# The second FFN of a two-layer vision block on one Trainium2 core: eight experts' probabilities spread by DMA, weighted inputs on GpSimd

## The chip, the core and the metric

The kernel runs on one core of a Trainium2 chip, in one launch, with fp32 data. The core has a matrix engine (TensorE, PE in the profile; PEld is its loading of weights), VectorE (DVE), ScalarE (ACT), GpSimd (POOL), and SyncE (SP), which here does nothing but issue DMA transfers. Every engine works through its own queue in a fixed order and waits at an instruction until its inputs and its buffer are ready. The metric is the device time of the whole kernel in microseconds, median of three runs.

## What is computed

The reference is a network of two layers on an input of 8 images with 128 channels and 64 x 64 points. Layer 0 is a four-way selective scan and a mixture of 64 experts. Layer 1 is a cascade of small state-space blocks with a convolutional FFN, and then, on the tokens, a mixture of eight experts. Only the end of layer 1 matters here:

```python
h1 = jnp.einsum('bchw,oc->bohw', out, fc1_w) + fc1_b[None, :, None, None]
dw = jax.lax.conv_general_dilated(h1, dw_w, (1, 1), 'SAME', ...)   # 3 x 3, each channel alone
h2 = jax.nn.gelu(dw + dw_b[None, :, None, None])
ffn = jnp.einsum('bohw,co->bchw', h2, fc2_w) + fc2_b[None, :, None, None]
return out + ffn
...
def _L1_ffn_ref(x, router_w, router_b, expert_w, expert_b):        # x: normalised tokens
    router_probs = jax.nn.softmax(x @ router_w + router_b, axis=-1)
    top_p, top_i = jax.lax.top_k(router_probs, 2)
    top_p = top_p / jnp.sum(top_p, axis=-1, keepdims=True)
    expert_out = jnp.einsum('bnd,edc->bnec', x, expert_w) + expert_b
    gathered = jnp.take_along_axis(expert_out, top_i[..., None], axis=2)
    return jnp.einsum('bnk,bnkc->bnc', top_p, gathered)
```

The kernel computes all eight experts for every token, with a probability of zero for the six that are not chosen: output = sum over e of (x * p_e) W_e, plus the biases weighted by p.

## The kernel before

`second_ffn` does the convolutional FFN and the mixture in one software pipeline. Its unit is a tile of 128 channels x 512 tokens (`S`), 64 of them (8 images of 8 tiles). A list `steps` gives each stage a delay in tiles; at every tick the stages run from the last to the first, each on another tile:

- `load` fetches `ys`, `seed` and `x2` (named `x` in the profile) from DRAM;
- `center`, `scale`: a norm (products `ln_m`, `ln_v` with the mean matrix; VectorE subtracts, giving `xc`; ScalarE squares, giving `sq`; GpSimd multiplies), and GpSimd adds into `seed`;
- `hidden`: product `h_p`, which ScalarE moves into rows `h`;
- `taps`: the 3 x 3 convolution as 18 VectorE instructions into two PSUM banks `dw`;
- `feed`: ScalarE's gelu, product `f_p`, VectorE and GpSimd add, giving `res`;
- `center2`, `scale2`: the second norm, giving `yn`;
- `logits`: four products of `yn` with the router for each tile into one PSUM bank `lg`, which holds a group of four tiles (`RS`). After the fourth, `route` reads the bank (`e<-lg_p`) and finds the two largest of eight and their normalised weights `pw` in some twenty small VectorE instructions;
- `weights`, for one tile: four transposes (`pt_p`, in the same bank `lg`), ScalarE copies them to rows 0 to 7 of `pT`; four rows are stored to DRAM (`p_d`) and read back spread over 128 partitions (`pb`, 1 MB);
- `weighted`: GpSimd multiplies `yn` with each of the four spread rows, giving four tiles `xwd`;
- `experts`: a bias product from `pT`, then eight products summed in bank `o_p`. For experts 0 to 3 the probability is spread by a product `pb_p` with a selection matrix `sel8`, and VectorE multiplies `yn` with it (`xw`); experts 4 to 7 use `xwd`. The two kinds alternate. VectorE adds `o_p` to `res`, and SP stores it.

All DMAs are issued by SP, in one order. The framework puts each engine's instructions in order by a plan with its own costs, so the order on an engine is not that of the source: tiles of different stages are mixed. A pool with `bufs=n` has n buffers by name, and an instruction that needs one waits until the earlier user is done. The bank `lg` has one buffer. The logits of a group occupy it over four tiles, and only when `route` has read it can the transposes of the group before go, so the work of `weights` comes in bursts of four tiles.

In the profile most VectorE and GpSimd instructions carry the lines of helpers (L335 `tt`, L341 `ts`, L344 `stt`), products L288, ScalarE L296; the names of tiles tell them apart.

Of the kernel before, what the change touches and what calls it, by code (L numbers as in the profile page):

```python
# [9 lines left out]
F32 = mybir.dt.float32  # L10
BF16 = mybir.dt.bfloat16
AF = mybir.ActivationFunctionType
ALU = mybir.AluOpType
# [10 lines left out]
S = 512  # L24
# [245 lines left out]
def bc(ap, n, axis=None):  # L270

    axis = len(ap.shape) if axis is None else axis
    v = ap.unsqueeze(axis)
    shape = list(v.shape)
    shape[axis] = n
    return v.to_broadcast(shape)


class Net:
# [809 lines left out]
    def ssd_project(self, cfg, W, ring, stk, n_tok, wk, ps):  # L1089
# [3 lines left out]
        nc = self.nc  # L1093
        NP, G, nh, hd, hi, ds = cfg.np, cfg.g, cfg.nh, cfg.hd, cfg.hi, cfg.ds
        g2, NH, gh, pb, pz = cfg.g2, cfg.nhalf, cfg.gh, cfg.pb, cfg.pz
# [8 lines left out]
        silus = []  # L1104
        BC = wk.tile([pb, NP, 2, n_tok], F32, name=f"BC_{t_}", bufs=nb_)
        per = min(NP, S // n_tok)
        for j0 in range(0, NP, per):
            p = ps.tile([128, 2, S], F32, tag="a", bufs=self.wide, name="bc_p")
# [8 lines left out]
        p = ps.tile([128, 2, S], F32, tag="a", bufs=self.wide, name="z_p")  # L1117
        for j in range(NP):
            o = (j * g2 % gh) * hi
            self.mm(p[o : o + g2 * hi, j * g2 // gh, :n_tok], Wp[:, cfg.o_z : cfg.o_z + g2 * hi], stk(j))  # L1120
        silus.append(self.act(zs, p[:pz, :NH, :n_tok], AF.Silu))
        yield None
        tok = wk.tile([128, NC, NP, cfg.wsil], F32, name=f"tok_{t_}", bufs=nb_)
        dtr = wk.tile([128, NC, NP, g2 * nh], F32, name=f"dtr_{t_}")
# [213 lines left out]
    def second_setup(self, pool, ps):  # L1338
        nc = self.nc

        self.sel8 = pool.tile([128, 8, 128], F32, name="sel8")
        nc.vector.tensor_copy(self.sel8, bc(self.k("ident")[:, :8], 128))
        self.pT = [pool.tile([128, S], F32, name=f"pT{q}") for q in range(4)]
        for t in self.pT:
            nc.vector.memset(t, 0.0)
        with self.tc.tile_pool(name="stw", bufs=1) as sp:
            spread = sp.tile(list(self.A["spread"].shape), F32, name="spread32")
            nc.sync.dma_start(spread, self.A["spread"])
            self.spread = pool.tile(list(self.A["spread"].shape), BF16, name="spread")
            nc.vector.tensor_copy(self.spread, spread)  # L1350
            self.st = sp.tile(list(self.A["stacked"].shape), F32, name="st")
            nc.sync.dma_start(self.st, self.A["stacked"])
            self.ssw = [self.ssd_weights(pool, CM, 0), self.ssd_weights(pool, CM, 1), self.ssd_weights(pool, SM, 0)]

        cr = self.w("cross")[:8]
        m = pool.tile([8, 1], F32, name="cr_m")
        nc.vector.tensor_reduce(m, cr, AX.X, ALU.max)
        cw = pool.tile([8, 8], F32, name="cr_w")
        self.ts(cw, cr, m, ALU.subtract)
        self.act(cw, cw, AF.Exp)  # L1360
        nc.vector.tensor_reduce(m, cw, AX.X, ALU.add)
        nc.vector.reciprocal(m, m)
        self.ts(cw, cw, m, ALU.mult)
        p = ps.tile([128, S], F32, tag="b", name="cr_p")
        self.mm(p[:, :8], self.k("of_q")[:8], cw)
        self.mix = pool.tile([128, 8, 16], F32, name="mix")
        self.tt(self.mix, bc(p[:, :8], 16), bc(self.k("same_c"), 8, 1), ALU.mult)
# [258 lines left out]
    def second_ffn(self):  # L1626


        nc, tc = self.nc, self.tc
        pool = nc.gpsimd  # L1630
        NP = 4
        RS = 4
        NQ = RS * S // 128
        total = self.nb * NS
        made = [{} for _ in range(total)]
        routed = {}
        with tc.tile_pool(name="ff", bufs=1) as pl, tc.tile_pool(name="ffw", bufs=2) as wk, \
# [14 lines left out]
            def place(n):  # L1652
                s = n % NS
                return n // NS, s, slice(s * S, (s + 1) * S)

            def bank(tag, bufs, name):
                return ps.tile([128, S], F32, tag=tag, bufs=bufs, name=name)

            def tile_(name, bufs):
                return wk.tile([C, S], F32, name=name, bufs=bufs)  # L1660
# [129 lines left out]
            def weights(n):  # L1790
                if n % RS == 0:
                    routed["now"] = routed["pw"]
                p = bank("lg", 1, "pt_p")
                for c in range(S // 128):
                    nc.tensor.transpose(p[:8, c * 128 : (c + 1) * 128], routed["now"][:, n % RS * (S // 128) + c, :],
                                        self.k("ident"))
                pT = self.pT[n % len(self.pT)]
                nc.scalar.copy(pT[:8], p[:8])
                d = self.dp.tile([NP, S], F32, name="p_d", bufs=3)
                nc.sync.dma_start(d, pT[8 - NP : 8])  # L1800
                made[n]["pb"] = wk.tile([128, NP, S], F32, name="pb", bufs=2)
                nc.sync.dma_start(made[n]["pb"], bc(d, 128, 0))

            def weighted(n):
                v = made[n]
                v["xw"] = []
                for e in range(NP):
                    xw = tile_("xwd", 2 * NP)
                    self.tt(xw, v["yn"], v["pb"][:, e], ALU.mult, pool)
                    v["xw"].append(xw)  # L1810

            def experts(n):
                v = made[n]
                b, s, sg = place(n)
                pT = self.pT[n % len(self.pT)]
                o = bank("o", 1, "o_p")
                self.mm(o, self.w("expert_b"), pT, start=True, stop=False)
                for g in range(8):

                    e = g // 2 + g % 2 * NP  # L1820
                    if e < 8 - NP:
                        pb = bank("pb", 1, "pb_p")
                        self.mm(pb, self.sel8[:, e, :], pT)
                        xw = tile_("xw", 3)
                        self.tt(xw, v["yn"], pb, ALU.mult)
                    else:
                        xw = v["xw"][e - 8 + NP]
                    self.mm(o, self.w("expert_w")[:, e * 128 : (e + 1) * 128], xw, start=False, stop=g == 7)
                x = v["res"]
                self.tt(x, x, o, ALU.add)  # L1830
                nc.sync.dma_start(self.out[b][:, sg], x)
                made[n] = None


            steps = [(0, load), (1, center), (2, scale), (3, hidden), (5, taps), (6, feed), (7, center2), (8, scale2),
                     (9, logits), (10 + RS, weights), (12 + RS, weighted), (13 + RS, experts)]
            for t in range(total + steps[-1][0]):
                for at, step in reversed(steps):
# [64 lines left out]
```

## Time and profile before

| | |
|---|---|
| median of 3 runs | 18365.06 us (18352.45 to 18369.7) |
| the profiled execution | 18370.72 us |
| its span | 18368.8 us |
| granted TensorE clock, mean | 0.954 |
| busy over the span | PE 86%, DVE 83%, ACT 61%, POOL 51% |
| second FFN, from 16814 to 18369 us | 1555 us |
| busy in it | PE 1372, DVE 1239, ACT 743, POOL 650 us |
| DMA share in it | 0.26 |

The second FFN is the last 8.5% of the span. A line of a window table gives the stretch, its length, then for PE, PEld, DVE, ACT and POOL the busy time and the number of instructions, then the granted clock, the DMA share and GB/s. A line of a group gives source line, engine, operation, tiles (out<-in), shapes and count, then busy us and the mean ns of one, then the idle time of the engine ahead of them and what ended it. A product of fp32 data appears as two records, and the count of a row counts records. A line of waits gives who waited for whom, us in total, how often, and the longest. A line of the timeline gives start, length, engine, source line, operation and tiles.

### The profile page before, as it was taken

The page shows a single profiled execution, that of the slowest core. Times are in us where ns is not written, and L with a number is a line of the kernel's source. Part 1 is how long each engine was busy: PE and PEld are TensorE (multiplying, and loading weights), DVE is VectorE, ACT ScalarE, POOL GpSimd, SP SyncE. Part 2 cuts the span into 40 slices and gives each one's busy share as a digit, 9 for nine tenths or more (in the row PEclk, how much of TensorE's full clock was granted, in tenths as well). Part 3 has the DMA queues.
Part 4 walks back from the last instruction along what each step waited for, and adds up shares of the span by engine and source line. Part 5 has one row for each costly group of instructions (what it writes and reads, how often), then busy time and mean ns, then how long its engine had stood idle before and what let it go on. Part 6 is the DMA issues. An engine that isn't in the chain of part 4 may idle for free. (4 is left out here: it accounts for less than half of the span.)

```text
span 18368.8 us, 300240 instructions
## 1 busy us (share of the span) xinstructions
PE 15729.2 (86%) x114341; PEld 8435.2 (46%) x114341; DVE 15174.0 (83%) x20453; ACT 11208.4 (61%) x15902; POOL 9306.3 (51%) x6308
## 2 busy tenths in 40 slices
PE   7777777787777778776887999999999999998998
PEld 2222222222222222223644677777777777774443
DVE  7999999999999999998264677777777777777886
ACT  5656666565666656554253667776777767676553
POOL 7878788787878878774011222222222222222444
PEclk9999999999999999998698999999999999998999
DMA  4555555555455555553442111111111111111222
GB/s 131 143 144 147 145 145 143 143 144 146 143 144 146 142 146 145 143 138 112 140 146 68 28 31 30 30 31 31 31 29 31 31 31 29 31 31 40 93 95 82
DMA packets 843742, 1734.86 MB, mean 94 GB/s; under 512 B 184315, under 2 KB 416667, under 8 KB 833883
## 3 DMA queue, kind: packets, MB, share of 16 engines
q1 hardware_dynamic: 842302, 1715.66, 32.6%
q8 instruction: 904, 14.81, 0.3%
q14 instruction: 536, 4.39, 0.1%
HBM read 1474.28 MB, written 241.04 MB: 93 GB/s over the span
## 5 line engine op out<-in xcount | busy, mean ns | idle before, releaser
L335 POOL TENSOR_TENSOR bx<-xE,B 128x1024 f32<-128x1024 f32 x2048 | 4811.6, 2359 | 320.8 <-DMA xE<-dtx_d 161.8
L288 PE MATMUL dA<-parts,expand 128*128 128x512 bf16 x12288 | 3194.6, 399 | 1719.2 <-DVE last L347 1301.2
L296 ACT ACTIVATE dA<-dA,negA 128x1024 f32<-128x1024 f32 x2048 | 2229.8, 1089 | 2948.9 <-PE dA L288 2942.4
L765 DVE TENSOR_TENSOR_SCAN dA<-dA,last,bx 128x1024 f32<-128x1024 f32 x1536 | 3609.7, 2350 | 91.1 <-ACT dA L296 81.3
L288 PEld LDWEIGHTS <-expand 128*128 128x128 bf16 x12288 | 1128.1, 100 | 4140.1 <-DVE last L347 2110.4
L344 DVE SCALAR_TENSOR_TENSOR E_cm<-E_cm,gm_cm 128x1024 f32<-128x1024 f32 x2048 | 2440.5, 1227 | 280.2 <-ACT E_cm L296 267.6
L335 DVE TENSOR_TENSOR hc<-dA,C 128x1024 f32<-128x1024 f32 x2048 | 2508.2, 1225 | 107.8 <-DVE dA L765 1.8
L1279 POOL COPY Sd_cm<-S_cm 64x128 f32<-64x128 f32 x1024 | 882.7, 862 | 2622.5 <-DVE S_cm L335 2533.1
L296 ACT ACTIVATE E_cm<-ss_p 128x1024 f32<-128x1024 f32 x2048 | 1981.5, 1021 | 266.0 <-PE ss_p L288 253.1
L335 POOL TENSOR_TENSOR xD_cm<-tok_cm,D_cm 128x256 f32<-128x256 f32 x512 | 404.5, 790 | 2374.0 <-PE y_p L288 2306.8
L288 PE MATMUL y_p<-E_cm,pad_cm 128*32 128x128 f32 x32768 | 1321.3, 277 | 119.6 <-DVE E_cm L344 118.6
L765 DVE TENSOR_TENSOR_SCAN dA<-dA,bx 128x1024 f32<-128x1024 f32 x512 | 1172.3, 2290 | 50.5 <-ACT dA L296 42.9
L288 PE MATMUL ss_p<-ssB_cm,ssA_cm 128*128 128x512 bf16 x4096 | 1090.5, 383 | 71.9 <-DVE gm_cm L335 44.2
L288 PE MATMUL y<-hc,kt 128*32 128x512 f32 x8192 | 1087.7, 651 | 3.6 <-DVE hc L335 3.6
L288 PEld LDWEIGHTS y_p<-E_cm,pad_cm 128*32 128x32 f32 x32768 | 903.7, 110 | 369.1 <-DVE E_cm L344 202.5
L288 PE MATMUL bc_p<-stk_cm,W_cm 128*128 128x256 f32 x4096 | 943.2, 384 | 26.4 <-DMA stk_cm<-xs 20.8
L1136 DVE COPY dtr_cm<-tok_p 128x16 f32<-128x16 f32 x1024 | 176.8, 173 | 867.1 <-ACT tok_cm L296 867.1
L288 PEld LDWEIGHTS bc_p<-stk_cm,W_cm 128*128 128x128 f32 x4096 | 770.8, 191 | 167.3 <-issue 28.4
L288 PE MATMUL tok_p<-W_cm,stk_cm 128*128 128x200 f32 x4096 | 749.5, 336 | 0.0
L344 DVE SCALAR_TENSOR_TENSOR dw<-h,w_second,dw 128x512 f32<-128x512 f32 x1024 | 723.1, 748 | 1.5 <-ACT h L296 1.1
L296 ACT ACTIVATE tok_cm<-tok_p 128x384 f32<-128x384 f32 x1024 | 503.1, 491 | 345.5 <-DVE dtr_cm L1136 183.0
L288 PEld LDWEIGHTS tok_p<-W_cm,stk_cm 128*128 128x128 f32 x4096 | 683.1, 190 | 52.2 <-ACT BC_cm L296 48.5
(432 smaller groups left out, 29590.8 us busy)
## 6 DMA issues: line engine op xcount, KB each, us to landing
xE<-dtx_d SPq DMA_DIRECT2D x2048, 512.0 KB
dtx_d<-dtx SPq DMA_DIRECT2D x256, 256.0 KB
x<-x SPq DMA_DIRECT2D x256, 256.0 KB
pb<-p_d SPq DMA_DIRECT2D x64, 1024.0 KB
ssA_cm<-cs_cm SPq DMA_DIRECT2D x3072, 4.0 KB
stk_cm<-xs SPq DMA_DIRECT2D x368, 128.0 KB
stk_cm<-y SPq DMA_DIRECT2D x368, 128.0 KB
px<-r SPq DMA_DIRECT2D x64, 256.0 KB
```

What stands on the lines that cost most here:

```text
L288: return self.ordered(self.nc.tensor.matmul(out, lhsT=lhsT, rhs=rhs, start=start, stop=stop))
L296: i = self.ordered(self.nc.scalar.activation(out, in_, func, **kw))
L335: self.ordered((eng or self.nc.vector).tensor_tensor(out, a, b, op))
L344: self.ordered(self.nc.vector.scalar_tensor_tensor(out=out, in0=a, scalar=s, in1=b, op0=op0, op1=op1))
L765: self.ordered(nc.vector.tensor_tensor_scan(out=t, data0=t, data1=bx.pop(n), initial=0.0 if ch["j"] == 0 else last[:, q : q + 1], op0=ALU. ...
L1136: nc.vector.tensor_copy(dtr[:, c, jj, :], v[:, :, cfg.wsil :])
L1279: nc.gpsimd.tensor_copy(Sd[gr, :, g * hi : (g + 1) * hi], S2[gr])
```

## The change

All eight probabilities are stored to DRAM and spread by two loads of 1 MB per tile, each of four experts, into three buffers where there were two of 1 MB for a whole tile. GpSimd makes the weighted inputs of experts 0 to 6, VectorE that of expert 7, ahead of the products. The ten buffers `xwd` replace eight `xwd` and three `xw`. The products `pb_p`, VectorE's multiplications from PSUM and the selection matrix go. The products run over the experts in the order 7, 0, 1, ... 6.

```diff
 def second_setup(self, pool, ps):
-    self.sel8 = pool.tile([128, 8, 128], F32, name="sel8")
-    nc.vector.tensor_copy(self.sel8, bc(self.k("ident")[:, :8], 128))
...
 def second_ffn(self):
-    NP = 4
+    NP = 7
...
         def weights(n):
...
-            d = self.dp.tile([NP, S], F32, name="p_d", bufs=3)
-            nc.sync.dma_start(d, pT[8 - NP : 8])
-            made[n]["pb"] = wk.tile([128, NP, S], F32, name="pb", bufs=2)
-            nc.sync.dma_start(made[n]["pb"], bc(d, 128, 0))
+            d = self.dp.tile([8, S], F32, name="p_d", bufs=3)
+            nc.sync.dma_start(d, pT[:8])
+            made[n]["pb"] = [wk.tile([128, 4, S], F32, name="pb", bufs=3) for _ in range(2)]
+            for i, t in enumerate(made[n]["pb"]):
+                nc.sync.dma_start(t, bc(d[4 * i : 4 * i + 4], 128, 0))
 
         def weighted(n):
             v = made[n]
             v["xw"] = []
-            for e in range(NP):
-                xw = tile_("xwd", 2 * NP)
-                self.tt(xw, v["yn"], v["pb"][:, e], ALU.mult, pool)
+            for e in range(8):
+                xw = tile_("xwd", 10)
+                self.tt(xw, v["yn"], v["pb"][e // 4][:, e % 4], ALU.mult, pool if e < NP else nc.vector)
                 v["xw"].append(xw)
 
         def experts(n):
...
             self.mm(o, self.w("expert_b"), pT, start=True, stop=False)
             for g in range(8):
-
-                e = g // 2 + g % 2 * NP
-                if e < 8 - NP:
-                    pb = bank("pb", 1, "pb_p")
-                    self.mm(pb, self.sel8[:, e, :], pT)
-                    xw = tile_("xw", 3)
-                    self.tt(xw, v["yn"], pb, ALU.mult)
-                else:
-                    xw = v["xw"][e - 8 + NP]
-                self.mm(o, self.w("expert_w")[:, e * 128 : (e + 1) * 128], xw, start=False, stop=g == 7)
+                e = (g + 7) % 8
+                self.mm(o, self.w("expert_w")[:, e * 128 : (e + 1) * 128], v["xw"][e], start=False, stop=g == 7)
```

## The prediction

> **What bounds the kernel now.** All that changes lies in the second FFN, which runs from about 16814 us to the end at 18368.8; the built order of every engine is the same up to there, but for one copy. So I left the shares of the whole span alone and read that stage: first the busy time of each engine in windows of one routing group (four tiles), then the groups by shape, the waits of VectorE, and the timeline.
>
> The windows, with the columns us, PE, weight loads, VectorE (DVE), ScalarE (ACT), GpSimd (POOL), granted clock, DMA share, GB/s:
>
> ```profile
> 17334.00:17420.00 86.00, 80.14 (x218) 36.09 (x217) 77.92 (x126) 46.59 (x77) 41.27 (x38) 1.00 0.30 100
> 17420.00:17507.00 87.00, 79.71 (x218) 35.91 (x217) 78.18 (x125) 45.79 (x73) 40.55 (x34) 1.00 0.29 98
> 17507.00:17596.00 89.00, 82.81 (x217) 37.04 (x216) 77.80 (x125) 46.61 (x77) 40.60 (x36) 0.96 0.28 94
> 18202.00:18350.00 148.00, 127.16 (x308) 50.03 (x308) 40.34 (x70) 6.23 (x11) 47.66 (x38) 0.99 0.22 75
> ```
>
> In the steady part TensorE (80 of 87 us) and VectorE (78) are both nearly full, and GpSimd has half its time free (41). In the last window only experts are left, and TensorE alone is the limit. The first reading of a group's logits, `e<-lg_p`, starts at 17027.19 for the second group and at 18161.14 for the fifteenth: 13 periods of 87.2 us. From there to the end it is 207.7 us.
>
> The groups by shape over the stage:
>
> ```profile
> L335 POOL TENSOR_TENSOR xwd<-yn,pb 128x512 f32<-128x512 f32 x256 | 327.3, 1291 | 304.0 <-PE o_p L288 138.7 <-issue 129.7 <-DMA pb<-p_d 32.0
> L288 PE MATMUL pb_p<-pT,sel 128*128 128x512 f32 x512 | 264.1, 597 | 0.0
> L335 DVE TENSOR_TENSOR xw<-yn,pb_p 128x512 f32<-128x512 f32 x256 | 175.2, 684 | 166.6 <-PE pb_p L288 164.8
> ```
>
> The second and third rows are removed, three quarters as many again join the first. A product is two records; in the timeline records follow each other at 0.43 us, so a product costs TensorE 0.86 us. VectorE's instructions overlap a little too: 0.62 us from start to start for `xw`.
>
> VectorE's waits over eight groups, 17248 to 17950:
>
> ```profile
> DVE xw L335 <- PE pb_p L288: 33.7, 58, 6.9
> DVE dw L341 <- ACT gelu L296: 32.9, 26, 4.0
> DVE res L335 <- PE o_p L288: 6.4, 8, 0.8
> DVE res L344 <- PE f_p L288: 4.1, 24, 0.2
> ```
>
> The first goes with the change; the rest, 5.4 us per group, stays. Last, how one burst starts, and how VectorE and GpSimd meet:
>
> ```profile
> 17729.37 0.28 DVE L335 TENSOR_TENSOR e<-lg_p,w_second 128x128 f32<-128x128 f32 x1
> ...
> 17735.81 1.39 SPq L1802 DMA_DIRECT2D pb<-p_d  x2
> ...
> 17736.51 0.28 DVE L335 TENSOR_TENSOR q<-q,kt 128x128 f32<-128x128 f32 x1
> ...
> 17740.38 5.06 POOL L335 TENSOR_TENSOR xwd<-yn,pb 128x512 f32<-128x512 f32 x4 [2.43 <-DMA pb<-p_d]
> ...
> 17741.73 1.25 DVE L335 TENSOR_TENSOR m<-m,m 128x16 f32<-128x16 f32 x1
> ...
> 17744.15 1.43 DVE L335 TENSOR_TENSOR q<-q,kt 128x128 f32<-128x128 f32 x1
> ```
>
> The logits' bank is free at 17729.37, four transposes, a copy and two DMAs follow, and GpSimd starts 11.0 us later, 4.6 us after the 1 MB load was issued. And `q<-q,kt` takes 0.28 us beside an idle GpSimd and 1.43 us beside its burst.
>
> **The change, per group of four tiles.**
>
> *TensorE* loses 16 products: 16 x 0.86 = 13.8 us of 80.0 (the first two windows, at full clock), leaving 66.2.
>
> *VectorE* loses 16 `xw`: 16 x 0.62 = 9.9 of 78.0, leaving 68.1. It gains four multiplications with both inputs in SBUF, which the trace of before has at this size nowhere in this stage. Nearest in size is `xw` itself, 0.62 each: 2.5 us. Against this stands the Trainium skill, "SBUF — State Buffer", section "Who interferes with whom": a VectorE instruction with two SBUF inputs and a GpSimd one that reads SBUF shut each other out for a whole instruction. The rows `m<-m,m` and `q<-q,kt` show just that, so an `xwd` on VectorE waits on average half of GpSimd's 1.28 us first: 0.64 + 0.62 = 1.26 each, 5.0 us. By the row alone the group is 2.5 us shorter, 33 us over 13 groups. I take 5.0, since GpSimd is now busy back to back where the four lie. VectorE then has 73.1 busy; with the 5.4 us of waits that stay, 78.5.
>
> *GpSimd* gains 12 x 1.28 = 15.4, and up to 4 x 0.6 in which VectorE holds it up: 41 becomes 59 of 87. As a share this is cover enough, but it comes as a burst of 28 from one start. In the built order the first 14 stand together, with other work (`res`, `ys`, `seed`, `yn`) between the rest. Started 11 us after the logits, tile one is done at 11 + 7 x 1.28 = 20, tile two at 29, tile three near 42, tile four near 56, each before TensorE comes to it after the pause below, so I cost the burst at nothing; uncovered, each us per tile would be 4 per group.
>
> *The pause.* The experts' order now begins with expert 7, VectorE's. In the built order VectorE makes that product for the group's first tile at the end of the routing arithmetic, just ahead of the last `pw<-pw,m`; before, that one starts 22 us after `e<-lg_p`. TensorE reaches its first expert product after 3.4 us, eight 512-column products (6.9), 16 transposes (2.4) and eight logits products (2.4), at 15 us. So it stands for about 6.6 us once a group, with everything behind it: `f_p`, `h_p`, `ln_m`. VectorE goes on with `dw` meanwhile and needs none of them at once. TensorE's path is 66.2 + 6.6 = 72.8, plus some 3 us of waits for `gelu` that it has now (25.5 us in eight groups): 76. A pause of 1.9 us came with a clock of 0.96 in the third window above; a longer one may cost another 1.7 us (2% of 87): 78.
>
> *DMA and SP's queue.* The 8 KB store becomes 16 KB; per tile one 1 MB load becomes two, which costs only where they land late. In the windows DMA is 0.29 busy; 64 more loads of 1 MB join some 140 MB of the stage (1555 us at 90 GB/s): near 0.45. The three half buffers hold one and a half tiles, so five of the eight loads of a group wait in SP's queue for GpSimd or VectorE to use up an earlier half, and the loads of `ys`, `seed` and `x` wait behind them, at worst until tile three's first half is used (near 40 us). ScalarE's next `ys` is wanted near 49 us, and a load behind 1 MB needs 4.6 us: 45. It is covered by some 4 us; cost nothing, uncovered see below.
>
> *The paths together.* VectorE's 78.5 and TensorE's 78 lean on each other, so I add little to the longer: 79 us, against 87.2. Thirteen periods give 13 x 8.2 = 107 us.
>
> *The end.* From 18161.14 twelve tiles of experts are left in both orders. Before: 207.7 us, 14.5 per tile at the end. After: 11 us, 28 GpSimd products (35.8), five other GpSimd instructions (6.4), VectorE's holds (2.4), the sum and its reading (2.4): 58. Then the last group's logits are read, 11 us again to the first product, and eight tiles at GpSimd's pace, 7 x 1.27 + 0.6 = 9.5 each, 76 (TensorE needs 9 x 0.86 = 7.7 of it), and 4 to the last store: 149. That is 59 us less. With the removed copy (0.6 us) the sum is 107 + 59 + 1 = 167 us.
>
> The profiled execution took 18370.72 us, its span 18368.8; the sum is made against these. The median of the runs, 18365.06, lies 5.7 below, well within the 17 us between its own runs. So 18365 - 167 = **18198 us**.
>
> **Rivals.** *Tighter:* the lock seldom bites and the pause is used up by work that VectorE is late with; the period is VectorE's 68.1 + 2.5 + 4 of waits, 75. Then 13 x 12.2 + 59 = 218: 18147. For it: VectorE, not TensorE, had the least slack left. Against: the row of 1.43 us. *The pause spreads:* in-order engines hand a stop of 6.6 us on, VectorE then waits for `f_p` and `ln_m`, and both waits are paid: 73.1 + 5.4 + 6.6 = 85. Then 13 x 2.2 + 55 = 84: 18281. For it: before, each group has 87.2 us where the fullest engine needs 80. *Slower:* the loads of `ys` held behind the half buffers come too late. Each stops ScalarE, and with it `gelu` and `dw`. The longest wait of GpSimd for a `pb` load is now 5.2 us; three of them per group on the path give 79 + 15.6 = 94.6, 13 x 7.4 - 55 = 41 slower: 18406. It decides once late loads cost over 12 us a group. Against it: covers of 4 us, and loads landing in 4.6 us at a DMA share of 0.45. *Nothing gained:* the products were hidden anyway. That would need a third bound, and none is seen: GpSimd and ScalarE are under 60%.
>
> **How the numbers follow.** The forecast has 0.58 (its own range 18165 to 18245), the tighter case 0.15, the spreading pause 0.17, the slower case 0.07, nothing gained 0.03. A change under 0.2% (37 us) can't be told from none here. From these, faster 0.89, within 0.2% 0.03, slower 0.08. The range reaches from the tighter case to past the spreading pause: 18130 to 18300.
>
> **What would show it.** Right: periods between the `e<-lg_p` of 77 to 81 us; VectorE's `xwd` near 1.2 us; TensorE idle for 5 to 8 us before `o_p` once a group, released by VectorE; tiles 9.5 us apart at the end with GpSimd full. Wrong: VectorE idle for `f_p` or `o_p` by over 8 us a group (the pause spreads), ScalarE waiting for `ys` DMAs by over 5 us a group (the queue), `xwd` on GpSimd well over 1.3 us (the lock costs GpSimd), or tiles at the end more than 10 us apart (half buffers too few).

## The result, and the profile after

The change makes the kernel slower: 18423.62 us (median of 6 runs, 18420.29 to 18430.25) against 18360.6 us of the kernel before in the same series. The ratio is 1.0034, with a 95% interval of 1.0023 to 1.0045. The forecast was 18198 us.

The profiled execution has a span of 18420.5 us, 51.7 more than before. The starts of `e<-lg_p` divide it into three parts. "First" is the start of the second group, "period" is the mean of the 13 periods from there to the fifteenth group, "tail" is from there to the end:

```
                first      13 periods       period   tail    span
before          17027.2    1133.9           87.2     207.7   18368.8
after           17015.2    1229.8           94.6     175.5   18420.5
forecast                                    79       149
```

So the periods cost 95.9 us more and the tail 32.2 us less; ahead of the second group lie the other 12.0. Over all profiled runs of this study "first" lies between 17010 and 17034 with no relation to the edit, so I don't explain those 12 us. From the second of the 13 periods of the changed kernel on, ten in a row take 95.5 to 95.7 us: a rhythm, where the kernel before varied between 85 and 92 in twelve of them and had 79.9 in the last.

The windows of the changed kernel, with the same columns as before; the last window is its tail, where only experts are left:

```profile
17334.00:17420.00 86.00, 67.91 (x171) 30.15 (x169) 73.78 (x103) 42.25 (x72) 46.05 (x38) 0.86 0.34 119
17420.00:17507.00 87.00, 71.89 (x172) 31.49 (x172) 73.06 (x99) 42.72 (x70) 47.43 (x42) 0.87 0.35 124
17507.00:17596.00 89.00, 71.14 (x161) 31.60 (x162) 75.02 (x100) 40.37 (x66) 53.13 (x43) 0.83 0.34 121
18260.00:18400.00 140.00, 100.80 (x236) 43.51 (x237) 63.84 (x52) 10.58 (x17) 97.99 (x78) 0.86 0.49 176
```

TensorE is no longer full (68 to 72 of 86 to 89 us) and its granted clock has fallen from about 1.0 to 0.85. VectorE's instructions fell from 125 to about 100 per window, but its busy time only from 78 to 74: the mean one has become dearer. The two rows of the products, by shape over the whole stage, say which:

```profile
L335 POOL TENSOR_TENSOR xwd<-yn,pb 128x512 f32<-128x512 f32 x448 | 572.8, 1315 | 147.1 <-PE o_p L288 131.8 <-DMA pb<-p_d 15.1
L335 DVE TENSOR_TENSOR xwd<-yn,pb 128x512 f32<-128x512 f32 x64 | 229.3, 3583 | 97.5 <-PE o_p L288 92.4 <-DMA pb<-p_d 5.1
```

GpSimd's products kept their price, 1.3 us. VectorE's 64 products took 3.58 us each where the forecast had 1.26. That is 229 us of VectorE instead of 81. The profile counts it as busy time, so no wait shows it. VectorE's four products of one group, and a part of what GpSimd did in the same time, from the timeline:

```profile
17610.67 1.12 DVE L335 TENSOR_TENSOR xwd<-yn,pb 128x512 f32<-128x512 f32 x1
17620.09 3.41 DVE L335 TENSOR_TENSOR xwd<-yn,pb 128x512 f32<-128x512 f32 x1 [1.79 <-PE o_p L288]
17633.89 8.96 DVE L335 TENSOR_TENSOR xwd<-yn,pb 128x512 f32<-128x512 f32 x1
17662.03 0.68 DVE L335 TENSOR_TENSOR xwd<-yn,pb 128x512 f32<-128x512 f32 x1
```

```profile
17604.75 18.20 POOL L335 TENSOR_TENSOR xwd<-yn,pb 128x512 f32<-128x512 f32 x14
...
17633.67 1.29 POOL L335 TENSOR_TENSOR seed<-seed,ys 128x512 f32<-128x512 f32 x1
17634.90 6.18 POOL L335 TENSOR_TENSOR xwd<-yn,pb 128x512 f32<-128x512 f32 x5
17641.02 1.28 POOL L335 TENSOR_TENSOR yn<-xc,sq 128x512 f32<-128x512 f32 x1
17651.20 1.30 POOL L335 TENSOR_TENSOR xwd<-yn,pb 128x512 f32<-128x512 f32 x1 [8.90 <-PE o_p L288]
```

The third product starts 0.22 us after GpSimd's `seed`. GpSimd runs seven instructions back to back until 17642.30; VectorE's product ends at 17642.85, 0.55 us later, close to the 0.68 us that the fourth product takes alone. The second ends 0.55 us after the end of the run of 14 (17622.95). The fourth, beside an idle GpSimd, takes 0.68. The first got in after the GpSimd instruction that was under way. Together they take 14.2 us, against the 5.0 of the forecast.

What is late next is seen in VectorE's waits, 17248 to 17950 (7.35 periods), and in TensorE's lines of the same group, an excerpt of the timeline:

```profile
DVE res L344 <- PE f_p L288: 58.3, 22, 5.3
DVE xc L335 <- PE ln_m L288: 24.7, 8, 3.5
DVE xwd L335 <- PE o_p L288: 12.8, 7, 1.9
DVE dw L341 <- ACT gelu L296: 3.1, 7, 0.4
```

```profile
17611.84 9.93 PE L288 MATMUL o_p<-xwd,w_second 128*128 128x512 f32 x16 [3.30 <-DVE xwd L335]
...
17627.49 7.03 PE L288 MATMUL o_p<-xwd,w_second 128*128 128x512 f32 x16
...
17644.95 2.07 PE L288 MATMUL o_p<-pT,w_second 128*128 128x512 f32 x2 [7.61 <-DVE res L335]
...
17664.12 1.19 PE L288 MATMUL ln_m<-res,kt 128*128 128x512 f32 x1 [3.53 <-ACT sq L296]
```

Behind the held product VectorE's `res<-res,o_p` is late, so the bank `o_p` is not free and TensorE stands for 7.61 us. GpSimd, out of `xwd` buffers, then waits 8.90 us for TensorE. Its `res`, `ys` and `seed` stand behind that product, ScalarE's next `ys` (its load waits for the buffer that `seed` frees, and is issued at 17659.95) and TensorE's `ln_m` behind those, and in the end VectorE waits for `f_p`: 58.3 us in these 7.35 periods, where it was 4.1 in eight groups before.

### The profile page after: what moved, and what is told of

It reads as the page before. It is cut to its first block, busy times and chain, and to the rows that moved or that the text cites. A ratio compares the mean times of both kernels' runs of the same rounds, so it can differ in the third digit from the quotient of the medians.

```text
span 18420.5 us, 298289 instructions
## 1 busy us (share of the span) xinstructions
PE 15539.6 (84%) x112772; PEld 8386.8 (46%) x113829; DVE 15224.8 (83%) x20260; ACT 11193.5 (61%) x15900; POOL 9542.5 (52%) x6500
## 4 chain that ended last, share of the span: by engine, by line
PE 27%; DVE 13%; ACT 5%; issue 3%; POOL 1%; DMA 1%; SPq 0%; DVEq 0%; another core or an unknown queue 0%; POOLq 0%; ACTq 0%
PE y_p L288 5%; PE bc_p L288 5%; PE tok_p L288 4%; PE ss_p L288 3%; DVE E_cm L344 3%; ACT L327 2%; PE o_p L288 2%; PE yo_s_p L288 2%; DVE dw L344 1%; PE z_p L288 1%; PE eA_p L288 1%; DVE gm_cm L335 1%; DVE xwd L335 1%; PE g_p L288 1%; ACT tok_cm L296 1%
## 5 line engine op out<-in xcount | busy, mean ns | idle before, releaser
L288 PE MATMUL ss_p<-ssB_cm,ssA_cm 128*128 128x512 bf16 x3582 | 1039.8, 383 | 110.3 <-DVE gm_cm L335 43.6
```

The costliest lines, as they stand in the source:

```text
L288: return self.ordered(self.nc.tensor.matmul(out, lhsT=lhsT, rhs=rhs, start=start, stop=stop))
```

## The experiments

All ratios are against the kernel before in the same series. Where an edit changes how many products an engine makes, their order or a load's queue, the plan also moves other instructions; in the run with the bank of 0.5 in the changed order, in those with the `ys` loads earlier in it and in the changed kernel, and with the products cut in two, the four compute engines keep the order of the kernel that was edited. Periods are read from the `e<-lg_p` of the profiled execution, as above.

### One SBUF input instead of two

```diff
+            half = ps.tile([128, S], F32, tag="half", bufs=1, name="half")
+            nc.vector.memset(half, 0.5)
...
-                    self.tt(xw, v["yn"], v["pb"][e // 4][:, e % 4], ALU.mult, pool if e < NP else nc.vector)
+                    if e < NP:
+                        self.tt(xw, v["yn"], v["pb"][e // 4][:, e % 4], ALU.mult, pool)
+                    else:
+                        self.tt(xw, v["yn"], half, ALU.mult)
```

> The changed kernel, but VectorE's product for expert 7 multiplies yn by a PSUM bank filled once with 0.5 instead of by the spread probability in SBUF: same operation, same size, same place in the order of every engine, one SBUF input instead of two. It leaves out the probability of expert 7. Theory A (VectorE with two SBUF inputs waits out GpSimd's whole back-to-back burst): VectorE's four products per group, 14.2 us together in the period I read after the change, fall to about 0.62 each, 2.5 us; the period of a group falls from 95.6 us to between 80 and 86, and the time to 18230 to 18310 us. Theory B (the half buffers and SP's queue bring the ys loads late, about 10 us a group of ScalarE's waits): the products get short but the period stays over 92 and the time at 18390 to 18425 us, because loads and GpSimd's burst are as before. Theory C (TensorE's stop for expert 7 at the head of a tile): the stop depends on when VectorE reaches the product, which the lock moves only in part; period 88 to 92, time 18320 to 18380 us.

Measured: 18247.6 us, ratio 0.9933 (0.9919 to 0.9948); period 84.0, tail 140.0. The rows of VectorE's product and the windows of this kernel:

```profile
L335 DVE TENSOR_TENSOR xwd<-yn,half 128x512 f32<-128x512 f32 x64 | 43.6, 682 | 88.7 <-PE o_p L288 88.7
```

```profile
17334.00:17420.00 86.00, 75.75 (x190) 34.16 (x189) 71.28 (x114) 46.88 (x78) 55.85 (x49) 0.88 0.43 148
17420.00:17507.00 87.00, 76.40 (x191) 34.70 (x192) 71.94 (x114) 48.03 (x79) 55.18 (x44) 0.87 0.42 146
```

The order on the four compute engines is that of the changed kernel. On SP one store a group stands ahead of a `ys` load instead of behind it, and the product no longer needs its `pb` half; GpSimd's waits for `pb` loads are about the same in both, 15.1 and 16.5 us over the stage. The span falls by 176.1 us, 138.0 of it in the 13 periods and 35.5 in the tail. This is the cost of the second SBUF input, with all that follows from it, and it is more than the kernel lost. Theory A holds; B and C don't.

### The same in a kernel that computes everything

```diff
-                    self.mm(o, self.w("expert_w")[:, e * 128 : (e + 1) * 128], v["xw"][e], start=False, stop=g == 7)
+                    if e < NP:
+                        xw = v["xw"][e]
+                    else:
+                        pb = bank("pb", 1, "pb_p")
+                        self.mm(pb, bc(self.k("ident")[:, e : e + 1], 128)[:, 0, :], pT)
+                        xw = tile_("xwd", 10)
+                        self.tt(xw, v["yn"], pb, ALU.mult)
+                    self.mm(o, self.w("expert_w")[:, e * 128 : (e + 1) * 128], xw, start=False, stop=g == 7)
```

> The changed kernel with expert 7's probability spread by a product into PSUM as before the change (TensorE +0.86 us a tile) and multiplied by VectorE there; seven halves of the work stay with GpSimd and the DMA loads stay as they are. The selector is the identity's column read with a step of zero, and xw takes its buffers from xwd's. Theory A: VectorE's product has one SBUF input and isn't locked out; the period is 80 to 86 us, 18230 to 18310 us. Theory B: the DMA loads and the burst are unchanged; period over 92, 18390 us or more. Theory C: TensorE now stops for VectorE at the head of each of four tiles (pb_p, product, o_p), up to 4 x 2 us more; period 86 to 92, 18310 to 18380 us.

Measured: 18271.25 us, ratio 0.9947 (0.993 to 0.9963); period 82.5, tail 164.7: Theory A again. VectorE's product from PSUM:

```profile
L335 DVE TENSOR_TENSOR xwd<-yn,pb_p 128x512 f32<-128x512 f32 x64 | 43.5, 679 | 5.2 <-PE pb_p L288 5.2
```

So spreading one of eight experts by TensorE, 0.86 us a tile, gains 152 us over the changed kernel, with the order that the plan then makes.

With two experts spread by products and six by DMA, on top of that edit:

```diff
-        NP = 7
+        NP = 6
...
-                    e = (g + 7) % 8
+                    e = (7, 0, 1, 2, 6, 3, 4, 5)[g]
```

> As the run with expert 7 spread by a product, with two experts (6 and 7) by products into PSUM and VectorE, six by DMA and GpSimd, TensorE's order 7 0 1 2 6 3 4 5. Per group TensorE has 80.0 - 8 x 0.86 = 73, VectorE 78 - 8 x 0.62 = 73, GpSimd 41 + 8 x 1.28 = 51. Theory A: no lock in the products, a shorter burst; period 79 to 84 us, 18200 to 18280 us, faster than both kernels. Theory B: one quarter less held in the half buffers does little; period 90 to 95, 18370 to 18420 us.

Measured: 18260.97 us, ratio 0.9939 (0.9924 to 0.9954); period 82.6, tail 160.8. Theory A's range holds. Both kernels beat the one before and the changed one; between the two of them the intervals decide nothing. Here TensorE keeps its clock:

```profile
17334.00:17420.00 86.00, 79.38 (x211) 36.22 (x209) 75.04 (x123) 48.42 (x80) 52.19 (x45) 0.96 0.42 151
17420.00:17507.00 87.00, 79.41 (x213) 36.54 (x212) 75.23 (x124) 51.28 (x86) 52.93 (x42) 0.96 0.41 149
```

### All eight on GpSimd

```diff
-        NP = 7
+        NP = 8
```

> The changed kernel with all eight products on GpSimd, none on VectorE. GpSimd gets 4 x 1.28 = 5.1 us more per group, and its first burst is 16 instructions. The order on the engines shifts somewhat with it. Theory A (lock): the period falls to 80 to 88 us, since only the small two-input instructions of the routing still meet the burst; 18230 to 18330 us. Theory B (half buffers, queue): a longer burst frees the halves later; period 95 to 100, 18410 to 18480 us. Theory C (TensorE's stop waits for VectorE): it now waits for GpSimd instead, shorter; period 88 to 92. At the end a tile takes 8 x 1.28 = 10.2 us on GpSimd.

Measured: 18357.87 us, ratio 0.9994 (0.9984 to 1.0003); period 89.5, tail 163.5. The lock of the products is gone, but 5.5 us a group of its gain are not there: A missed by 1.5 us of period, and the period is what C had. The waits of TensorE, 17248 to 17950, and one of these stops in the timeline:

```profile
PE o_p L288 <- POOL xwd L335: 46.8, 7, 7.8
```

```profile
17400.42 13.84 POOL L335 TENSOR_TENSOR xwd<-yn,pb 128x512 f32<-128x512 f32 x11 [0.32 <-DMA pb<-p_d]
...
17410.60 9.73 PE L288 MATMUL o_p<-xwd,w_second 128*128 128x512 f32 x16 [6.65 <-POOL xwd L335]
```

That is one stop of nearly 7 us a group, in a kernel with no VectorE product at all. TensorE starts 10.2 us after GpSimd, which is eight products of 1.27: its order still begins with expert 7, and GpSimd makes that one last of a tile's eight. So a burst on an engine that is half idle as a whole can still stop TensorE; how much would be left with another order of the experts was not run.

### Expert 7 last

```diff
-                    e = (g + 7) % 8
+                    e = g
```

> The changed kernel with the experts in the order 0 to 7, so that VectorE's product comes last in each tile instead of first. Theory A (lock): VectorE is locked out as long as before, only TensorE meets it later; the period stays at 92 to 97 us, 18380 to 18440 us. Theory C (TensorE's stop at the head of the tile decides): TensorE does seven products while VectorE waits; period 85 to 89, 18280 to 18340 us.

Measured: 18375.29 us, ratio 1.0006 (0.9997 to 1.0016); period 90.4, tail 175.9. Between A and C, in the range of neither: the sum of VectorE's products stays (223.1 us over the stage), while 4 us a period are gained. The longest holds of all are here, one of 17.08 us at 17683.01 and this one of 16.77 us, beside the run of GpSimd that follows (starts and durations; seven rows of 19 instructions, of which 14 overlap it):

```profile
17136.56 16.77 DVE L335 TENSOR_TENSOR xwd<-yn,pb 128x512 f32<-128x512 f32 x1
```

```profile
17129.28 11.25 POOL L335 TENSOR_TENSOR xwd<-yn,pb 128x512 f32<-128x512 f32 x9
17140.47 1.29 POOL L335 TENSOR_TENSOR res<-res,x 128x512 f32<-128x512 f32 x1
...
17149.06 3.72 POOL L335 TENSOR_TENSOR xwd<-yn,pb 128x512 f32<-128x512 f32 x3
```

It ends at 17153.33, 0.55 us after the last of them.

The same order without the lock (the bank of 0.5 and `e = g`):

> The run whose VectorE product reads one SBUF input and a PSUM bank of 0.5 (it leaves out expert 7's probability), with the experts in the order 0 to 7: no lock in the products and no stop for VectorE at the head of a tile. Its neighbour has 84.0 us a group, TensorE 73.9 busy at a clock of 0.87 and about 10 us of stops. If the stop at the head is what I still pay, the period falls to 78 to 81 us, 18170 to 18215 us, with the clock back over 0.95; if the stops come from ScalarE and ln_m, it stays at 82 to 86 and 18225 to 18270 us.

Measured: 18297.32 us, ratio 0.9966 (0.9955 to 0.9977); period 87.8, tail 136.8. Both expectations missed: without the stop at the head the period is 3.8 us longer than with it. TensorE's largest wait has another cause, GpSimd's `yn` behind the products in GpSimd's queue:

```profile
PE lg_p L288 <- POOL yn L335: 56.3, 17, 4.9
```

So moving the stop away from the head of a tile does not bring the forecast. The plan moves many other instructions here, so what that stop costs in the 84.0 us is not shown; the place of the products in GpSimd's queue does cost, as these waits show.

### Twice as many products of two SBUF inputs

```diff
-        NP = 7
+        NP = 6
...
-                    e = (g + 7) % 8
+                    e = (g + 6) % 8
```

> The changed kernel with two products per tile on VectorE from SBUF (experts 6 and 7) and six on GpSimd. Theory A (lock): the second product stands right behind the first and is locked out again where GpSimd still has instructions ready; per group 4 to 12 us more on VectorE, less what a burst shorter by one instruction per tile gives back: period 97 to 106 us, 18450 to 18560 us. Theory B (GpSimd's burst and its half buffers are what costs): GpSimd has 5.1 us less per group and frees the halves sooner; period 90 to 94, 18340 to 18400 us.

Measured: 18283.59 us, ratio 0.9957 (0.9942 to 0.9971); period 85.5, tail 160.7. I expected slower and it is 140 us faster than the changed kernel; B's numbers are missed too. The row of the product over the stage:

```profile
L335 DVE TENSOR_TENSOR xwd<-yn,pb 128x512 f32<-128x512 f32 x128 | 169.1, 1353 | 62.1 <-PE o_p L288 47.2 <-DMA pb<-p_d 11.6 <-POOL xwd L335 3.3
```

Twice the instructions take less in sum (169 instead of 229 us), since in this order they seldom meet a long run of GpSimd's: of the 104 in the 13 periods one takes over 5 us, where 13 of 52 did. The price of such a product is not a constant that could be multiplied by a count.

### The loads of ys

In the run with the bank of 0.5, ScalarE still waits 10.4 us a group for loads of `ys`. First I put them on ScalarE's queue, there and in the changed kernel:

```diff
-                    nc.sync.dma_start(v[name], src[b][:, sg])
+                    (nc.scalar if name == "ys" else nc.sync).dma_start(v[name], src[b][:, sg])
```

> The run whose VectorE product reads one SBUF input and a PSUM bank of 0.5 (it leaves out expert 7's probability), and in addition the loads of ys are issued by ScalarE's queue instead of SP's, so that they don't stand behind the pb loads that wait for a half buffer. In that run 84.0 us a group are left against my 79, with 10.4 us a group of ScalarE's waits for ys DMAs. If the queue holds the 5 us, the period falls to 78 to 81 us and the time to 18180 to 18210 us. If these waits lie beside other work (the engines wait for one another in turn), the period stays at 83 to 84.5 and the time at 18235 to 18260 us.

> The changed kernel with one edit: the loads of ys on ScalarE's queue. All products as changed. If the waits for ys (10 us a group) are a cost of their own, the period falls from 95.6 to between 88 and 92 us and the time to 18330 to 18380 us. If they are an echo of VectorE being locked out, the period stays at 94 to 96 and the time at 18400 to 18430 us, and the waits of ScalarE move to another releaser.

Measured: with the bank of 0.5 18344.73 us, ratio 0.9988 (0.9978 to 0.9997), period 90.9; in the changed kernel 18424.69 us, ratio 1.0034 (1.0023 to 1.0045), period 94.1. The edit did not do what I meant: ScalarE issues the load only when it comes to it, and then waits longer. In the run with the bank of 0.5 this was 142.8 us in 7.6 periods, 19 us a group:

```profile
ACT ys L296 <- DMA ys<-ys: 142.8, 31, 5.7
```

Without the lock some 8 us more of this wait come with a period 7 us longer. Beside the lock a similar rise, from 74 to 129 us in the same 702 us, costs nothing, as the echo was to look. In both runs the plan also moves instructions of TensorE, ScalarE and GpSimd, so what the wait alone costs is not shown.

Then the loads one tile earlier in SP's queue, for the run with the bank of 0.5, for the changed kernel and for the mix of six and two:

```diff
-                for name, src, bufs in (("ys", self.ys, 4), ("seed", self.seed, 7), ("x2", self.x2, 6)):
+                for m in range(n + (n > 0), min(n + 2, total)):
+                    made[m]["ys"] = tile_("ys", 5)
+                    nc.sync.dma_start(made[m]["ys"], self.ys[m // NS][:, place(m)[2]])
+                for name, src, bufs in (("seed", self.seed, 7), ("x2", self.x2, 6)):
...
-                v["yn"] = tile_("yn", RS + 7)
+                v["yn"] = tile_("yn", RS + 6)
```

> The run whose VectorE product reads one SBUF input and a PSUM bank of 0.5 (it leaves out expert 7's probability), with the loads of ys issued one tile earlier on SP's queue (five ys buffers instead of four, ten yn buffers instead of eleven). That run had 84.0 us a group and 10.4 us a group of ScalarE's waits for ys DMAs; putting those loads on ScalarE's own queue made the waits 18.6 us a group and the period 92. If these waits stand on the path one for one, taking them away gives back 5 to 9 us a group: period 75 to 79, 18115 to 18180 us, near what my sum had for the steady part. If VectorE's waits for f_p and ln_m only change their releaser, the period is 82 to 84 and the time 18215 to 18250 us.

> The changed kernel with the loads of ys one tile earlier and nothing else (five ys buffers, ten yn buffers). The ys waits are 10 us a group there, VectorE's locked products 14 us. If late loads are a cost of their own beside the lock, the period falls from 95.6 to 86 to 90 us, 18300 to 18360 us. If the lock sets the period alone and the late loads are its echo, the period stays at 94 to 96, 18405 to 18430 us.

> Six experts by DMA and GpSimd, two by products into PSUM and VectorE (period 82.6), with the loads of ys one tile earlier. There ScalarE's waits for ys DMAs were small, so I expect little from it: period 81 to 83, 18230 to 18265 us. If the loads matter there too, below 80 and under 18220 us.

Measured: 18240.1 us, ratio 0.9937 (0.9923 to 0.9952), period 83.3; 18374.1 us, ratio 1.0011 (1.0002 to 1.0021), its ten runs between 18339 and 18441; 18265.34 us, ratio 0.9949 (0.9934 to 0.9963), period 83.2. The first is in the range for waits that only change their releaser, the median of the second lies between its two ranges, the third is at the edge of the first of its two. In the first the waits for `ys` stayed (86.0 us in 702), because these loads wait for GpSimd's `seed` to free a buffer and not for the `pb` loads ahead of them. So this did not test what I wanted, and whether a removal of the waits would shorten the 84 us is not shown. The second has its profiled execution at the slow end (18440.86 us, periods of 95.6 us); its other nine runs lie between 18339 and 18395 us. The same program falls into the rhythm of 95.6 us in one execution and, by their times, stays mostly out of it in the others.

The mix with early loads once more, with four `pb` buffers of three experts, two whole tiles instead of one and a half:

```diff
-                made[n]["pb"] = [wk.tile([128, 4, S], F32, name="pb", bufs=3) for _ in range(2)]
+                made[n]["pb"] = [wk.tile([128, 3, S], F32, name="pb", bufs=4) for _ in range(2)]
...
-                    nc.sync.dma_start(t, bc(d[4 * i : 4 * i + 4], 128, 0))
+                    nc.sync.dma_start(t, bc(d[3 * i : 3 * i + 3], 128, 0))
```

> As the run before this one, with the spread probabilities in four halves of three experts instead of three halves of four (the same memory: two whole tiles instead of one and a half). GpSimd waited 8.8 us a group for pb loads in the run with two products. If the half buffers cost their own, those waits go and the period falls to 77 to 80 us, 18170 to 18230 us; if not, it stays at 81 to 83, 18230 to 18265 us.

Measured: 18262.17 us, ratio 0.9945 (0.9929 to 0.9962), period 82.2. GpSimd's waits for `pb` loads stayed as they were (70.4 us in 702, 73.0 with the half buffers and the same early loads), so it is not the third half that they wait for.

### The hold by itself, and what it depends on

A test behind the end of the changed kernel: runs of GpSimd products, and in them VectorE products of several sizes.

```diff
+                    for i in range(n):
+                        self.tt(g[i], last[:, :S] if i == 0 else a[:, :S], b[:, :S], ALU.mult, nc.gpsimd)
+                    for i in range(before):
+                        self.tt(pre, g[1] if i == 0 else a[:, :S], one, ALU.mult)
...
+                        self.tt(last[:, :w], x[:, :w], y, ALU.mult)
```

> The changed kernel with a test behind its end, each case twice: GpSimd multiplies 4, 8 or 14 tiles of 128x512 from SBUF back to back; VectorE, released by the second of them, makes one multiplication with one SBUF input (0.68 us) and then one or more with two SBUF inputs of 128, 256, 512 or 1024 elements a partition; in the last case with one input in PSUM. Theory 1 (a long VectorE instruction waits out the whole run): started about 3.3 us into the run, the 512 one takes about 2.4 us with 4 GpSimd instructions, 7.5 with 8 and 15.3 with 14, whatever stands before it, and the one of 128 gets in at the first boundary, 1.3 us or less. Theory 2 (one GpSimd instruction at most, what my prediction used): 0.7 to 2.0 us with each number of GpSimd instructions and each size. Theory 3 (it depends on what VectorE did just before): the cases with 512 differ from each other by what stands ahead of them. The control with PSUM takes 0.68 in all theories.

Measured: theory 2 in all cases but one. A 512 product started 0.58 us before the end of a GpSimd instruction takes 1.13 us, one right after another 1.63, one released directly 1.74, one of 128 columns 0.74, six in a row of 128 columns 1.23 each after the first, the control 0.68. The next GpSimd instruction pays for it with 1.71 instead of 1.26. The exception, in the second round of the first case, waited out the last two GpSimd instructions (2.35 us) where the first round had 1.13. So by itself the hold is one instruction long. But the runs of the test follow each other without a pause (GpSimd is busy for 274.7 of 276 us), so only that exception had the end of a run just ahead.

In the trace of the changed kernel I then counted VectorE's products that start inside a GpSimd run with more to come: 33 of them with seven or fewer GpSimd instructions left, that one included, before a pause; all 33 waited out the run. 18 had eight or more left; 17 of them got in at the next end of a GpSimd instruction, and one waited out all eight. Other runs do not follow this count: with expert 7 last, products with 8, 12 and twice 14 left waited out the run, and with two products a tile 15 of 35 with seven or fewer left got in earlier. In the routing arithmetic, small instructions got in nearly always, none over 1.4 us. Two runs asked whether the size decides, with the product cut into two and into four pieces:

```diff
+                    for j in range(0, S, S if e < NP else 256):
+                        c = slice(j, j + (S if e < NP else 256))
+                        self.tt(xw[:, c], v["yn"][:, c], v["pb"][e // 4][:, e % 4, c], ALU.mult,
+                                pool if e < NP else nc.vector)
```

> The changed kernel with VectorE's product for expert 7 cut into two instructions of 256 columns, nothing else; the order of TensorE and ScalarE is the same. In the stage nearly all VectorE instructions of 128 elements with two SBUF inputs get in after the GpSimd instruction that runs, while of the 512 ones those that meet the last seven or fewer GpSimd instructions before a stop wait for all of these. If the size decides, two pieces wait for one GpSimd instruction each, 1 to 1.5 us a piece, together at most 8 us a group instead of 14.2, none over 3 us; period 86 to 92, 18310 to 18390 us. If what GpSimd has before it decides, the first piece waits as long as the whole did (8 to 9 us in the same place); period 94 to 97, 18405 to 18440 us.

> As the run before, in four instructions of 128 columns, the size that does get in at a boundary elsewhere in this stage. If the size decides, each piece takes 0.3 to 1.3 us, a product beside GpSimd's run 4 to 5 us, the group 12 us or less, with no piece over 2 us; the period is 88 to 94. If the size doesn't decide, a first piece of 8 us or more is seen in the same place, and the period is 94 to 98.

Measured: 18424.56 us, ratio 1.0026 (1.0016 to 1.0037), and 18467.62 us, ratio 1.0057 (1.004 to 1.0074), the second with a period of 96.7. A first piece of 128 columns waits 8.60 us, in the place where the whole waited 8.96:

```profile
17651.07 8.60 DVE L335 TENSOR_TENSOR xwd<-yn,pb 128x128 f32<-128x128 f32 x1
```

```profile
17650.87 1.28 POOL L335 TENSOR_TENSOR seed<-seed,ys 128x512 f32<-128x512 f32 x1
17652.09 6.21 POOL L335 TENSOR_TENSOR xwd<-yn,pb 128x512 f32<-128x512 f32 x5
17658.28 1.25 POOL L335 TENSOR_TENSOR yn<-xc,sq 128x512 f32<-128x512 f32 x1
```

Size does not decide. Of the two pieces, nine of ten executions took 18419 to 18436 us and one, the profiled one, 18342.71: there only 5 of 128 pieces took over 5 us, and nine of the 13 periods were 85 to 88 us. One program, 80 us apart; that the nine are in the rhythm is read from their times alone.

Last, the test with what the stage has and the first test had not: GpSimd's run ends at an instruction that waits for ScalarE.

```diff
+                    if stop:
+                        for i in range(3 * n):
+                            self.ordered(nc.scalar.copy(w, w if i else g[0]))
+                        self.tt(g[n], w, b, ALU.mult, nc.gpsimd)
+                    self.tt(pre, g[k], one, ALU.mult)
+                    self.tt(last[:, :two], a[:, :two], c[:, :two], ALU.mult)
```

> The changed kernel with a second test behind its end, each case twice: GpSimd multiplies n tiles of 128x512 from SBUF back to back and then has an instruction that waits for a long chain of ScalarE, as it waits for another engine in the stage; VectorE, released by GpSimd's instruction number k+1, makes one multiplication with one SBUF input and then one with two. (n, k, columns): (4, 1, 512), (8, 1, 512), (14, 1, 512), (14, 8, 512), (14, 4, 512), (8, 1, 128), (8, 4, 512); the last case is (8, 1, 512) without the stop. Theory 4 (what counts is how much GpSimd has left before it must wait: with seven or fewer instructions all are ahead of VectorE, with more VectorE gets in at the next boundary): the cases with n = 4 and 8 wait out the whole run, 2.4 and 7.2 us, also with 128 columns; (14, 1) takes 1.1 to 1.8 us; (14, 8) waits out 5 us. Theory 2 (one GpSimd instruction at most): 0.7 to 1.8 us in every case.

Measured: theory 2, in all 16 cases: 1.13 or 1.14 us with 512 columns and 0.74 with 128. The case (8, 1, 512), VectorE first and GpSimd's run and stop after it:

```profile
18450.14 1.14 DVE L335 TENSOR_TENSOR llast<-la,lc 128x512 f32<-128x512 f32 x1
```

```profile
18448.24 9.06 POOL L335 TENSOR_TENSOR lg<-la,lb 128x512 f32<-128x512 f32 x7
18463.95 1.26 POOL L335 TENSOR_TENSOR lg<-lw,lb 128x512 f32<-128x512 f32 x1 [6.65 <-ACT lw L1852]
```

So few instructions left and a stop behind them do not make a hold. What lets GpSimd keep VectorE out over a whole run, in the stage and not in the tests, stays open. None of these does it alone: the size of VectorE's instruction, the length of the run (4 to 14), a stop at its end. Not tested is what else runs: TensorE and the DMA engines, idle in both tests (DMA share 0.00), are busy in the stage (0.37).

## Why the prediction was wrong

The span forecast was 18368.8 - 167 = 18201.8; it came to 18420.5, 218.7 more. The run with one SBUF input divides this: 176.1 us are the hold and its consequences, 42.6 us the rest.

- *VectorE's new work: the step that failed.* "so an `xwd` on VectorE waits on average half of GpSimd's 1.28 us first: 0.64 + 0.62 = 1.26 each, 5.0 us." Measured: 3.58 each over the stage, 14.0 us a group. The lock was named; its size was not. The Trainium skill, "SBUF — State Buffer", section "Who interferes with whom", lets the loser wait for the other engine's instruction, and the rows of before agreed (1.43 us beside a burst, 0.28 without). The tests agree with the page too (1.14 us). In the stage the measurement says otherwise, 8.96 us across 7 instructions in the changed kernel and up to 17.08 us across 14 with expert 7 last, and the measurement decides. I had taken the rows from the routing arithmetic at the head of a group; the four new products stand elsewhere, and only the first of them, in that place, cost what I said (1.12 us).
- *TensorE's loss of the products* was right: its records fall from 215 to 182 a group (counts below), 16 products of two.
- *The pause.* Forecast 6.6 us for VectorE at the first `o_p` of a group, measured 3.30 in the group shown. A stop of 7.61 for the `o_p` bank, behind the held product, came in its place.
- *The burst at nothing, and the queue at nothing.* Neither can be judged in the changed kernel, where the hold covers them. Without the hold, ScalarE waits 10 us a group for `ys`, but the two edits to these loads did not remove the wait. The burst does cost where it stands ahead of something: a stop of nearly 7 us for `o_p` where TensorE begins with GpSimd's eighth product, 7 us a group for `yn` with expert 7 last.
- *The sum of 79.* With the hold gone it is 84.0; over 13 periods that is 65 us. The window 17248 to 17950 of the kernel before and of the run with one SBUF input (8.36 periods), and VectorE's largest waits in the latter:

```profile
17248.00:17950.00 702.00, 649.70 (x1730) 291.93 (x1729) 620.51 (x994) 369.31 (x600) 325.18 (x273) 0.98 0.29 97
17248.00:17950.00 702.00, 617.60 (x1525) 276.41 (x1526) 580.23 (x924) 379.68 (x624) 449.26 (x373) 0.87 0.42 146
```

```profile
DVE res L344 <- PE f_p L288: 54.5, 17, 6.1
DVE xc L335 <- PE ln_m L288: 31.1, 13, 3.9
```

In the second, TensorE is busy 73.9 us a group and stands for 10.1. The stops are in sum what I had (6.6 + 3), though not the same ones. The busy time is not: at a granted 0.87 the 66.2 us of full clock take 7.7 more, where I allowed 1.7. These 6 us make 78 into 84. That is a sum that fits, not a test. The rival of the spreading pause, with 85, fits as well: VectorE stands 6.5 us a group for `f_p` and 3.7 for `ln_m`. No run separates the two. What pulls the clock down is open too: I had put the 0.96 of the third window to its pause of 1.9 us, but the first two windows hold stops of 1.83 and 2.02 us at 1.00. In the group of the changed kernel shown above the clock was 0.50 from 17606.4 to 17612.0 and 1.00 from 17627.5 to 17634.5, and sixteen records of `o_p` took 9.93 us from the end of the first stretch on and 7.03 in the second. In the mix of six and two, with TensorE busy for 79.4 of 86 us, it was 0.96.
- *The end.* Forecast 149, measured 175.5, and 140.0 without the hold. VectorE's 14 products from 18202 on took 4.0 us each and the last tiles came about 11 us apart instead of 9.5.
- *The rivals.* The slower case came nearest in time (18406), by luck: its mechanism was late loads, and none was needed. "ScalarE waiting for `ys` DMAs by over 5 us a group" did show, at 10 us, but as an echo: in the changed kernel a rise of this wait to 17 us changed nothing. The spreading pause showed as well (VectorE idle 8 us a group for `f_p`), behind the hold; without the hold its number fits, as said.

## What to carry to other kernels

Before giving VectorE an instruction with two SBUF inputs next to an engine that works through bursts of SBUF reads, price it by the whole run of that engine as the upper end, not by one instruction, or keep one input in PSUM: one product of TensorE, 0.86 us a tile, bought 152 us here. The profile counts time in which an instruction is held as busy time, so compare an instruction's mean with the shortest of the same shape before believing a busy share. And a lower busy sum on the fullest engine is worth less than it looks when its granted clock falls with it: 0.98 before, 0.87 with the products gone and the hold away.

## What the runs showed that I had not expected

- VectorE held out over a run of GpSimd instructions, 8.96 us over 7 and up to 17.08 us over 14, where tests of the same pair give 1.14 us, once 2.35.
- The hold goes with a rhythm: ten periods of 95.5 to 95.7 us in a row. The kernel with two pieces ran at 18419 to 18436 us in nine executions and at 18342.71 in one, with the same instructions in the same order.
- Twice the number of such products, in another order, cost less in sum, 169 against 229 us.
